# Four-layer scan network on one core: even slots' side work moved ahead of the third exponentials, step sizes made half a block sooner, first and last image's border work put beside the scans

## The chip, the core and the metric

The kernel runs on one core of a Trainium2 chip. A core has five engines that run their own instruction streams in order: TensorE (PE in the profile; its weight loads are PEld), VectorE (DVE), ScalarE (ACT), GpSimd (POOL), and SyncE (SP), which here issues all DMA transfers. Engines wait for each other through semaphores. An instruction that waits holds up everything behind it on its own engine. The metric is the device time of one execution in microseconds (us); lower is better.

## What is computed

Eight images of 48x48 positions and 96 channels pass through four residual layers, each applied to a group-normalized input:

```
x = x + L0(gn(x))   # two-dimensional selective scan, four directions ("ss2d")
x = x + L1(gn(x))   # spectral upsampling, MLP, downsampling
x = x + L2(gn(x))   # selective scans along every row and column ("lines")
x = x + L3(gn(x))   # two-dimensional selective scan again
```

A two-dimensional layer does, per image:

```
xc, z = split(x @ in_proj.T);  xc = silu(depthwise_conv3x3(xc) + conv_b)   # 192 channels
for each of 4 directions k (row-wise, column-wise, and both reversed):
    dts, B, C = split(x_proj[k] @ xs)                  # 6 + 16 + 16 rows
    delta = softplus(dt_proj[k] @ dts + dt_bias[k])
    h = h * exp(delta * A) + (delta * u) * B;  y = sum_n h * C    # 16 states per channel
y = layernorm(sum of the four directions + u * D) * silu(z);  out = y @ out_proj.T
```

The line layer has a four-tap convolution along the line, its own gate and projection per direction, and starts its state at zero on every line.

## The kernel before

**Stages.** `ss2d("l0")`, `spectral`, `lines` and `ss2d("l3")` follow one another. Both kinds of scan layer call the same `scans` (L166).

**Blocks, turns, slots.** Work is a list of blocks (L175): for each image (`job`), for each direction `k`, five pieces of the image, `BLKS`: four of 10 lines (480 columns) and one of 8 (384). A reversed direction takes them from last to first. In the two-dimensional layers directions 0 and 2 run along rows, 1 and 3 along columns; 2 and 3 are reversed. A block has 4 turns (q = 0 to 3), a turn two slots, an even one (2q) and an odd one (2q+1); so a block has `NG` = 8 slots and an image 160. A turn scans 6 units of 128 partitions (channel and state packed), in three scan instructions of two units each.

**A turn, engine by engine** (the loop at L348). ScalarE makes the decays `exp(delta*A)` for two units at a time (`make_da`, L255) into one of two PSUM buffers; a buffer comes free when the scan before last has read it. VectorE runs the three scans (L263) and the products `du*B` (`make_dbu`, L235) for later slots, reading B from one PSUM buffer that ScalarE fills (`copy_b`, L216). GpSimd takes a part of those products (L235), saves the carries between blocks (`keep`, L270) and multiplies the states by C (`make_hc`, L276). TensorE sums over states (`reduce`, L296 and L298); the first reduce of a half-block opens its PSUM group with an `opening` matmul (L292) that reads the running sum of directions, `ysum`. ScalarE copies the finished half back (`done`, L634).

**Side work.** `aside(at)` (L333) is called once in each slot. It issues the next block's loads (`load_bc` in slots 2, 3, 6, 7; `load_dd` in 4, 5), takes one step of the generator `side`, and runs the steps planned for this slot (`run`). In the odd slot it stands after the third scan. In the even slot it stands after the third `make_da`, after `copy_b` and after VectorE's product.

**Planned steps.** `plan(b, at)` (L306) enters the steps that `stage1(b)` returns under their slot numbers. For the two-dimensional layers (L619) these are: the projection to B, C and dts (s0, s1), the store of B and C to DRAM (s3), the two step-size matmuls and bias copies (s4, `biased`), Softplus (s6), `du` on GpSimd for two halves (L422), and two stores of step sizes and du to DRAM (`store_dd`, L410), from where `load_dd` (L192) broadcasts them over partitions. A block is planned two blocks ahead; s0 falls into slot 0, Softplus into slot 6, du into slots 7 and 0, the stores into 1 and 2. The tiles `dds` and `bcl` have one buffer each. Before the loop, 16 slots' worth of planned steps for two blocks run on their own.

**The generator `side` of `ss2d`** (L554): it loads the next image (L468), does `post` of the image before (L496: mean and variance over channels, then Sqrt and reciprocal of all variances, then scaling, gate, output projection and store, block by block), then `front` of the next image (group norm) and, from slot 80 on, `conv` (L470: nine taps on TensorE, one tap group a slot, and two Silu on ScalarE in every eighth slot, 7). For the first image `front` and the whole `conv` run ahead of the scans, and for the last image the whole `post` runs after them.

**The line layer's planned steps** (L774): convolution matmuls in slots 3 and 4, Silu in 6 (L729), step-size matmuls in 7, Softplus in 0 (L757), gate matmuls and du in 1, gate Silu in 2 (L771). So its ScalarE functions other than Exp all fall into even slots. Different functions need different tables, and a load of a table is an instruction of its own in the profile.

Of the kernel before, what the change touches and what calls it, by code (L numbers as in the profile page):

```python
# [16 lines left out]
L = H * W  # L17
# [58 lines left out]
def vss_stack_kernel(ctx: ExitStack, tc: tile.TileContext, i: dict, out: bass.AP):  # L76
# [86 lines left out]
        yield  # L163


    def scans(dirs, restart, a, pools, ps, stage1, opening, done, side, tail):  # L166

# [3 lines left out]


        blocks = [Block(job, k, blk, n == 0, n == len(BLKS) - 1, dirs[k][1])  # L175
                  for job in range(nb) for k in range(NK)
                  for n, blk in enumerate(range(len(BLKS))[::-1 if dirs[k][1] else 1])]
        for b in blocks:
            b.columns(restart)
# [168 lines left out]
        for t, (b, q) in enumerate(turns):  # L348
            at, nblk = 2 * t, t // (NG // 2)
            if q == 0:  # L350
                if nblk + 2 < len(blocks):
                    plan(blocks[nblk + 2], at)
                if b.k == 0 and b.first:
                    beside = side(b.job)
            scan(t, 0)
            if t > 0:
                keep(t - 1, 1)
                make_hc(t - 1, 1)
            make_dbu(at + 2, nc.vector)
# [19 lines left out]
            if q == NG // 2 - 1 and b.k == NK - 1 and b.last:  # L379
                for _ in beside:  # L380
                    while tail:
                        tail.pop(0)()
# [47 lines left out]
    def ss2d(l, xin, xout, b0=0):  # L430
# [36 lines left out]
        def load_x(b):  # L467
            nc.sync.dma_start(xpad[:C, 1:1 + H, 1:1 + W], seq(xin[b], False))  # L468

        def conv(b):  # L470
            us[b] = big.tile([DH, 2, L], F32, tag="big", name="u")
            zs[b] = zdr.tile([DH, 2, L], F32, tag="z", name="zd")
            for r0, nr in BLKS:
                n = nr * SEG
                for half in range(2):
                    pu = side_psum()
# [16 lines left out]
                    yield  # L493
                    nc.sync.dma_start(zs[b][:, half, s], z[:, :n])

        def post(b):  # L496
            y = yss[b]
            var = small.tile([CH, L // CH], F32, tag="var", name="var")
            for r0, nr in BLKS:
# [12 lines left out]
                pv = side_psum()  # L512
                for c in range(n // CH):
                    for half in range(2):
                        nc.tensor.matmul(pv[:CH, c:c + 1], lhsT=sq[:, half, c * CH:(c + 1) * CH], rhs=ones,  # L515
                                         start=(half == 0), stop=(half == 1))
                yield
                nc.vector.tensor_copy(var[:, r0 * W // CH:(r0 * W + n) // CH], pv[:CH, :n // CH])  # L518
                yield
            nc.scalar.activation(var, var, AF.Sqrt, bias=eps5[:CH])  # L520
            yield
            nc.vector.reciprocal(var, var)  # L522
            yield
            for r0, nr in BLKS:
# [124 lines left out]
    def lines(xin, xout):  # L649
# [169 lines left out]
        load_x(0)  # L819
        for _ in front(0):  # L820
            pass
        scans(dirs, True, a, pools, ps, stage1, opening, done, side, tail)
        stack.close()


# [286 lines left out]
```

## Time and profile before

| | us |
|---|---|
| median of 3 runs (lowest to highest) | 19550.73 (19544.21 to 19555.11) |
| the profiled execution, its own time | 19542.61 |
| its span, first to last instruction | 19540.6 |
| first scan of the first layer starts | 148.68 |
| first layer's scans, first to last | 148.7 to 5902.6 |
| last layer's scans, first to last | 13675.7 to 19432.6 |
| last scan to the end | 108.0 |

The mean granted TensorE clock was 0.744 of full speed. The page gives busy time by engine, costliest groups of instructions and who released them. A group's line reads: line of the kernel, engine, operation, output and inputs, shape, count, then busy time, mean duration in ns, then the idle time of the engine just before these instructions and the releasers that ended most of it. A timeline row reads: start, duration, engine, line, operation, tiles, count, and in brackets the idle time before it with its releaser. Idle time of an engine that is not the bottleneck costs nothing. The costliest ScalarE groups beside those shown in the prediction:

```profile
L255 ACT ACTIVATE ps_da<-dd,w_l_a 128x481 f32<-128x481 f32 (+3 forms) x11520 | 7414.7, 648 | 2729.7 <-DVE dbu L263 2523.7
L216 ACT COPY ps_b<-bc 128x480 f32<-128x480 f32 (+1 forms) x3360 | 1798.4, 535 | 300.7 <-DVE dbu L235 271.3
L255 ACT ACT_TABLE_LOAD x970 | 1244.5, 1283 | 17.1
```

### The profile page before, as it was taken

How to read it: one execution, taken by the hardware profiler on the slowest of the kernel's cores; microseconds unless marked ns; L12 is line 12 of the kernel's file. 1: busy time of each engine (PE TensorE's matmuls, PEld its weight loads, DVE VectorE, ACT ScalarE, POOL GpSimd, SP SyncE). 2: the span in 40 equal slices, each digit the busy share in tenths (PEclk: the TensorE clock that was granted, in tenths of full speed). 3: DMA queues.
4: the chain of work that ended last, by engine and by line, in shares of the span. 5: the costliest groups of instructions: out<-in, count | busy, mean ns of one | idle time of the engine just before them, and what ended most of it. 6: DMA issues, size and time to landing. Idle time of an engine off the chain costs nothing. (4 is left out here: it accounts for less than half of the span.)

```text
span 19540.6 us, 172984 instructions
## 1 busy us (share of the span) xinstructions
PE 15237.1 (78%) x53500; PEld 4370.8 (22%) x53500; DVE 16831.8 (86%) x11281; ACT 14144.5 (72%) x22222; POOL 16028.7 (82%) x9825
## 2 busy tenths in 40 slices
PE   6777777777767887888888988887677777777776
PEld 1211211211214552222222222222121121121121
DVE  6999999999992228999999999996999999999997
ACT  5877777877772227788788777885778778778775
POOL 6999999999991007888888888886999999999997
PEclk6777776776767777888878888887677677667765
DMA  3444444444443324434434444443444444444443
GB/s 130 160 162 158 162 160 163 158 163 158 156 170 48 50 45 145 145 141 150 150 139 147 147 146 145 144 149 112 158 163 160 159 164 157 160 162 161 156 165 123
DMA packets 768486, 2829.44 MB, mean 145 GB/s; under 512 B 235724, under 2 KB 298668, under 8 KB 640926
## 3 DMA queue, kind: packets, MB, share of 16 engines
q1 hardware_dynamic: 767558, 2818.38, 43.1%
q8 instruction: 422, 6.91, 0.1%
q14 instruction: 506, 4.15, 0.1%
HBM read 2371.42 MB, written 446.69 MB: 144 GB/s over the span
## 5 line engine op out<-in xcount | busy, mean ns | idle before, releaser
L263 DVE TENSOR_TENSOR_SCAN dbu<-ps_da,dbu 128x962 f32<-128x962 f32 (+3 forms) x5760 | 11858.2, 2071 | 897.9 <-ACT ps_da L255 895.7
L276 POOL TENSOR_TENSOR dbu<-dbu,bc 128x1440 f32<-128x1440 f32 (+1 forms) x3840 | 11439.8, 2985 | 1040.6 <-DVE dbu L263 814.0
L255 ACT ACTIVATE ps_da<-dd,w_l_a 128x481 f32<-128x481 f32 (+3 forms) x11520 | 7414.7, 648 | 2729.7 <-DVE dbu L263 2523.7
L296 PE MATMUL ps_y<-dbu,w_red 128*32 128x480 f32 (+1 forms) x23040 | 4983.6, 752 | 3051.0 <-POOL dbu L276 3047.3
L298 PE MATMUL ps_y<-dbu,w_red 128*32 128x480 f32 (+1 forms) x7680 | 4942.9, 752 | 0.0
L235 DVE TENSOR_TENSOR dbu<-dd,ps_b 128x1440 f32<-128x1440 f32 (+5 forms) x3840 | 4645.3, 1210 | 320.1 <-ACT ps_b L216 275.7
L235 POOL TENSOR_TENSOR dbu<-dd,bc 128x480 f32<-128x480 f32 (+3 forms) x1920 | 3026.2, 1576 | 61.9 <-DMA bc<-bcd 36.6
L296 PEld LDWEIGHTS ps_y<-dbu,w_red 128*32 128x32 f32 x23040 | 742.7, 125 | 7009.7 <-POOL dbu L276 5283.6
L216 ACT COPY ps_b<-bc 128x480 f32<-128x480 f32 (+1 forms) x3360 | 1798.4, 535 | 300.7 <-DVE dbu L235 271.3
L722 PE MATMUL ps_s<-xpad,w_l_cw 128*128 128x480 f32 (+1 forms) x2560 | 1747.2, 834 | 2.3 <-ACT xpad L124 1.6
L481 PE MATMUL ps_side<-xpad,w_l_cw 128*128 128x480 f32 (+1 forms) x2880 | 1617.4, 690 | 4.6 <-ACT xpad L124 4.5
L255 ACT ACT_TABLE_LOAD x970 | 1244.5, 1283 | 17.1
L113 POOL MEMSET w_l_cw<- 128x1760 f32 (+1 forms) x3 | 5.8, 1942 | 1326.7 <-DVE x L932 1321.3
L422 POOL TENSOR_TENSOR dds<-dds,u 96x480 f32<-96x480 f32 (+1 forms) x640 | 793.6, 1240 | 259.9 <-ACT dds L611 259.9
L593 PE MATMUL ps_s<-u,w_l_xp 96*38 96x480 f32 (+1 forms) x1280 | 957.2, 888 | 4.1 <-ACT dds L587 3.0
L583 PE MATMUL ps_s<-bcl,dtw 6*96 6x480 f32 (+1 forms) x1280 | 878.4, 775 | 86.3 <-ACT dds L587 82.2
L270 POOL COPY carry<-dbu 128x3 f32<-128x3 f32 x2048 | 386.4, 189 | 582.6 <-DVE dbu L263 570.2
L292 PE MATMUL ps_y<-ysum,w_ident 96*96 96x480 f32 (+1 forms) x960 | 740.7, 861 | 113.7 <-ACT ysum L634 112.8
L481 PEld LDWEIGHTS ps_side<-xpad,w_l_cw 128*128 128x128 f32 x2880 | 571.0, 222 | 1115.0 <-issue 916.4
L722 PEld LDWEIGHTS ps_s<-xpad,w_l_cw 128*128 128x128 f32 x2560 | 525.8, 210 | 1087.1 <-issue 938.1
L298 PEld LDWEIGHTS ps_y<-dbu,w_red 128*32 128x32 f32 x7680 | 683.1, 125 | 0.0
L763 PE MATMUL ps_s<-xpad,w_l_inz 96*96 96x480 f32 (+1 forms) x640 | 505.7, 924 | 86.9 <-ACT dds L757 69.2
(146 smaller groups left out, 12586.2 us busy)
## 6 DMA issues: line engine op xcount, KB each, us to landing
dd<-dd SPq DMA_DIRECT2D x512, 1443.0 KB
bc<-bcd SPq DMA_DIRECT2D x1536, 480.0 KB
dd<-dd SPq DMA_DIRECT2D x256, 1440.0 KB
dd<-dds SPq DMA_DIRECT2D x512, 360.8 KB
dd<-dd SPq DMA_DIRECT2D x128, 1155.0 KB
bc<-bcd SPq DMA_DIRECT2D x384, 384.0 KB
dd<-dds SPq DMA_DIRECT2D x256, 360.0 KB
dd<-dd SPq DMA_DIRECT2D x64, 1152.0 KB
```

Source lines behind the costliest of these rows:

```text
L216: nc.scalar.copy(bps[t][:, :b.n], bcs[t][:, 0, :b.n])
L235: engine.tensor_mul(o, du, by.unsqueeze(1).to_broadcast([P, hi - lo, b.n]))
L255: nc.scalar.activation(da[:, at:at + b.m], b.got[half][:, u % 3, 0, :], AF.Exp, scale=a[:, b.k, ci:ci + 1])
L263: nc.vector.tensor_tensor_scan(db, da, db, 0.0, ALU.mult, ALU.add)
L276: nc.gpsimd.tensor_mul(h, h, bcs.pop(2 * t + sub)[:, 1, :n].unsqueeze(1).to_broadcast([P, 3, n]))
L296: nc.tensor.matmul(y[32 * g:32 * g + 32, :n], lhsT=wc["red"][:, :32], rhs=hc[:, g, b.at], start=False, stop=(slot == 3))
L298: nc.tensor.matmul(y[DH:, :n], lhsT=wc["red"][:, 32:], rhs=hc[:, 2, b.at], start=(slot == 0), stop=(slot == 3))
L422: nc.gpsimd.tensor_mul(rows(du, n), rows(dt, n), u)
L481: nc.tensor.matmul(pu[:, :n], lhsT=flat[:, at:at + P], rhs=xpad[:, r0 + dy:r0 + dy + nr, dx:dx + W], start=(tap == 0), stop=(tap == 8))
L583: nc.tensor.matmul(got["p"][:DH, :n], lhsT=dtw[2 * NS:, b.k, half, :], rhs=b.bcl[2 * NS:, :n], start=True, stop=True)
L593: nc.tensor.matmul(got["p"][:NBC, :n], lhsT=w[f"{l}_xp"][:, b.k, half, :], rhs=u[:, half], start=(half == 0), stop=(half == 1))
L722: nc.tensor.matmul(got["u", half][:, :n], lhsT=flat[:, at:at + P], rhs=shifted(off), start=(tap == 0), stop=(tap == 3))
```

## The change

Five edits. In `scans`: (a) the order of directions becomes an argument; the two-dimensional layers use 0, 1, 3, 2, the line layer the old one. (b) Blocks are planned three ahead, with base slot `at + NG`, and three blocks' planned steps run before the loop instead of two. (c) In the even slot, `reduce` and `aside` move ahead of `copy_b`, the third `make_da` and VectorE's product. In `ss2d`: (d) the keys of `stage1` go down by four, so that each step falls four slots (half a block) earlier relative to its block's scans: s0 in slot 4, Softplus in slot 2, du in 3 and 4, stores in 5 and 6. In the line layer keys and base cancel, and steps keep their slots. (e) `conv` and `post` take a list of blocks. The first image's last convolution block goes into `side`, two steps a slot; the last image's `post` goes into `side` block by block for four of the five blocks, two steps a slot, each once its rows are complete, and only one block is left after the scans. Each such `post` has a Sqrt and a reciprocal of its own.

```diff
         blocks = [Block(job, k, blk, n == 0, n == len(BLKS) - 1, dirs[k][1])
-                  for job in range(nb) for k in range(NK)
+                  for job in range(nb) for k in order
...
-        for n, b in enumerate(blocks[:2]):
+        for n, b in enumerate(blocks[:3]):
             plan(b, NG * (n - 2))
-        for t in range(-2 * NG, 0):
+        for t in range(-3 * NG, 0):
             run(t)
...
             if q == 0:
-                if nblk + 2 < len(blocks):
-                    plan(blocks[nblk + 2], at)
-                if b.k == 0 and b.first:
+                if nblk + 3 < len(blocks):
+                    plan(blocks[nblk + 3], at + NG)
+                if b.k == order[0] and b.first:
                     beside = side(b.job)
...
             scan(t, 1)
-            make_da(t, 2)
-            copy_b(at + 3)
-            make_dbu(at + 3, nc.vector)
             if t > 0:
                 reduce(t - 1, 1)
             aside(at)
+            copy_b(at + 3)
+            make_da(t, 2)
+            make_dbu(at + 3, nc.vector)
             bring(t + 1)
...
         def side(job):
             used = 0
             more = job + 1 < nb
+            if job == 0:
+                for n, _ in enumerate(conv(0, BLKS[4:])):
+                    if n % 2:
+                        used += 1
+                        yield
             if more:
                 load_x(job + 1)
...
-                yield from conv(job + 1)
+                yield from conv(job + 1, BLKS)
+            else:
+
+                for n, blk in enumerate(BLKS[:0:-1]):
+                    while used < (NK * len(BLKS) - len(BLKS) + n + 1) * NG + 2:
+                        used += 1
+                        yield
+                    for m, _ in enumerate(post(job, [blk])):
+                        if m % 2:
+                            used += 1
+                            yield
...
-            return {0: s0, 1: s1, 3: s3, 4: s4, 5: lambda: biased(1), 6: s6, 7: du(0), 8: du(1),
-                    NG + 1: store(0), NG + 2: store(1)}
+            return {-4: s0, -3: s1, -1: s3, 0: s4, 1: lambda: biased(1), 2: s6, 3: du(0), 4: du(1),
+                    5: store(0), 6: store(1)}
...
-        for _ in conv(0):
+        for _ in conv(0, BLKS[:4]):
             pass
-        scans(dirs, False, a, pools, ps, stage1, opening, done, side, [])
-        for _ in post(nb - 1):
+        scans(dirs, (0, 1, 3, 2), False, a, pools, ps, stage1, opening, done, side, [])
+        for _ in post(nb - 1, BLKS[:1]):
             pass
```

More of the change, by code (lines that the diff above doesn't have):

```diff
@@ L163, in norm_scale, with scans @@
         yield
-    def scans(dirs, restart, a, pools, ps, stage1, opening, done, side, tail):
+    def scans(dirs, order, restart, a, pools, ps, stage1, opening, done, side, tail):
         blocks = [Block(job, k, blk, n == 0, n == len(BLKS) - 1, dirs[k][1])
-                  for job in range(nb) for k in range(NK)
+                  for job in range(nb) for k in order
                   for n, blk in enumerate(range(len(BLKS))[::-1 if dirs[k][1] else 1])]
@@ L378, in scans @@
             aside(at + 1)
-            if q == NG // 2 - 1 and b.k == NK - 1 and b.last:
+            if q == NG // 2 - 1 and b.k == order[-1] and b.last:
                 for _ in beside:
@@ L468, in load_x, with conv @@
             nc.sync.dma_start(xpad[:C, 1:1 + H, 1:1 + W], seq(xin[b], False))
[L470 to L473, printed above, removed]
+        def conv(b, blks):
+            if blks[0] == BLKS[0]:
+                us[b] = big.tile([DH, 2, L], F32, tag="big", name="u")
+                zs[b] = zdr.tile([DH, 2, L], F32, tag="z", name="zd")
+            for r0, nr in blks:
                 n = nr * SEG
@@ L494, in conv, with post @@
                     nc.sync.dma_start(zs[b][:, half, s], z[:, :n])
-        def post(b):
+        def post(b, blks=BLKS):
             y = yss[b]
             var = small.tile([CH, L // CH], F32, tag="var", name="var")
-            for r0, nr in BLKS:
+            v0, v1 = min(r0 for r0, nr in blks) * W // CH, max(r0 + nr for r0, nr in blks) * W // CH
+            for r0, nr in blks:
                 n = nr * SEG
@@ L519, in post @@
                 yield
-            nc.scalar.activation(var, var, AF.Sqrt, bias=eps5[:CH])
+            nc.scalar.activation(var[:, v0:v1], var[:, v0:v1], AF.Sqrt, bias=eps5[:CH])
             yield
-            nc.vector.reciprocal(var, var)
+            nc.vector.reciprocal(var[:, v0:v1], var[:, v0:v1])
             yield
-            for r0, nr in BLKS:
+            for r0, nr in blks:
                 n = nr * SEG
@@ L821, in lines @@
             pass
-        scans(dirs, True, a, pools, ps, stage1, opening, done, side, tail)
+        scans(dirs, range(NK), True, a, pools, ps, stage1, opening, done, side, tail)
         stack.close()
```

## The prediction

> **What bounds the kernel now.** I read the page first (busy shares, costliest groups), then VectorE's waits in the first scan stage, then timelines of single blocks, then both ends of a stage.
>
> ```profile
> PE 15237.1 (78%) x53500; PEld 4370.8 (22%) x53500; DVE 16831.8 (86%) x11281; ACT 14144.5 (72%) x22222; POOL 16028.7 (82%) x9825
> L263 DVE TENSOR_TENSOR_SCAN dbu<-ps_da,dbu 128x962 f32<-128x962 f32 (+3 forms) x5760 | 11858.2, 2071 | 897.9 <-ACT ps_da L255 895.7
> L276 POOL TENSOR_TENSOR dbu<-dbu,bc 128x1440 f32<-128x1440 f32 (+1 forms) x3840 | 11439.8, 2985 | 1040.6 <-DVE dbu L263 814.0
> ```
>
> VectorE (DVE) and GpSimd (POOL) carry the scan stages. What VectorE loses there is one wait, the scan for its exponentials (third number after the bar). The starts of every twelfth scan in the timeline give block times: in both two-dimensional stages a 480-column block takes 34.5 to 34.8 us without a convolution beside it (last image, second half), and 36.7 with one. VectorE's own work is 34.2 (turns of 8.3 and 8.8 us where no wait is shown); GpSimd's is 34.8 (timeline from 5633 us, where it is never idle: eight products at a pitch of 3.28 with their carry copy, four B products 6.3, two du 2.25). So GpSimd is the floor, 0.6 above VectorE, and a convolution block wastes 1.9. Here is one, on ScalarE (ACT) and VectorE:
>
> ```profile
> 2007.94 0.56 ACT L216 COPY ps_b<-bc 128x480 f32<-128x480 f32 x1 [0.18 <-DVE dbu L235]
> 2008.52 1.28 ACT L611 ACT_TABLE_LOAD   x1
> 2009.82 1.00 ACT L611 ACTIVATE dds<-dds 96x960 f32<-96x960 f32 x1
> 2010.93 1.28 ACT L255 ACT_TABLE_LOAD   x1
> 2012.22 1.36 ACT L255 ACTIVATE ps_da<-dd,w_l_a 128x481 f32<-128x481 f32 x2
> 2014.08 1.28 ACT L490 ACT_TABLE_LOAD   x1
> 2016.51 1.28 ACT L255 ACT_TABLE_LOAD   x1
> ```
> ```profile
> 2013.62 2.16 DVE L263 TENSOR_TENSOR_SCAN dbu<-ps_da,dbu 128x962 f32<-128x962 f32 x1 [0.53 <-ACT ps_da L255]
> 2019.20 2.16 DVE L263 TENSOR_TENSOR_SCAN dbu<-ps_da,dbu 128x962 f32<-128x962 f32 x1 [1.88 <-ACT ps_da L255]
> ```
>
> Softplus (slot 6) and the convolution's Silu (slot 7) follow each other, each with two table loads: the scans wait 0.53 and 1.88 us. In the line stage the waits are for Silu, Softplus, Silu in slots 6, 0 and 2, and TensorE (PE) is late:
>
> ```profile
> 9606.81 7.75 PE L722 MATMUL ps_s<-xpad,w_l_cw 128*128 128x480 f32 x8
> 9614.60 0.66 ACT L729 ACTIVATE ub<-ps_s,w_l_cb 96x480 f32<-96x480 f32 x1 [0.26 <-PE ps_s L722]
> ```
>
> The convolution of this column block ended 6.5 us after its turn's first scan (9608.08), and ScalarE, which came 5.6 us after it, still waited. At the ends of a stage nothing is hidden:
>
> ```profile
> 127.32 5.44 SPq L192 DMA_DIRECT2D dd<-dd  x2
> 132.30 0.66 ACT L587 ACTIVATE dds<-ps_s,w_l_dtb 96x480 f32<-96x480 f32 x1 [14.08 <-DMA dd<-dds]
> ```
> ```profile
> 19446.82 0.16 DVE L518 COPY var<-ps_side 96x5 f32<-96x5 f32 x1 [4.10 <-PE ps_side L515]
> 19483.02 0.16 DVE L518 COPY var<-ps_side 96x4 f32<-96x4 f32 x1 [3.75 <-PE ps_side L515]
> 19493.17 0.65 DVE L550 TENSOR_TENSOR xi<-xi,ps_side 96x480 f32<-96x480 f32 x1 [5.91 <-PE ps_side L547]
> ```
>
> **What the Trainium skill says.** "ScalarE: Activation LUTs", What ACT_TABLE_LOAD costs: a change of table set is 1283 ns plus a drain of 1380. The trace has the 1283 (1.28 above), not the drain: loads start 0.02 us after the copy before. "SBUF — State Buffer", SBUF: two separate sides: a VectorE instruction with two SBUF inputs and a GpSimd instruction exclude each other for their whole length. The trace agrees: L149, a 96x1 subtraction, takes 0.15 us with GpSimd idle and 2616 ns on average beside the scans. The pieces of post read one operand from PSUM, so I charge no lock. "DMA: Bandwidth & Descriptors", the SWDGE anatomy: most of a transfer's fixed 2 us is the write's receipt. Here the store of the step sizes costs block 1 a wait of 14.08 us, far more, and that number is used.
>
> **1. Softplus moved from slot 6 to 2 (plan a block earlier, keys four lower).** Convolution blocks: with no Softplus before it, the slot-7 chain starts when the second scan of turn 3 ends: from the start of the exponentials (2012.22) to the end of the next ones (2019.16) it is 6.95 us; the second scan of the next turn is naturally 6.6 after that start. Left: 0.4 instead of 0.53+1.88. In exchange Softplus now heads the even slot of turn 1: ScalarE ends the turn's second exponentials about 1.6 us (row blocks) to 2.0 (columns, whose ysum copy takes 0.97, not 0.55) after the first scan's start, as in turn 3 today (5624.42 against 5622.78); then load 1.29, Softplus 1.0, the B copy 0.5, load 1.29, exponentials 1.36: 5.45. The third scan is due at 6.72. Stall 0.3 to 0.7, in convolution blocks some 0.9 since ScalarE is still catching up. I add 0.2 for GpSimd's burst of du in turn 2, which holds TensorE's reduce and so the bcl copy. So 34.2+0.4+0.9+0.2 = 35.7: 1.0 saved per 480 block; the 384 block, 32.9 now, to 27.8 of VectorE's work and the same two stalls before shorter scans, 1.2 and 1.6, 30.6: 2.3; the first block of the next image 1.0. Eight, one and one: 11.3 per image, 7 images, 2 stages: **-158**. Bounds: 0 (stall only moved) to 21 per image (GpSimd's floor). The moved steps' stores come along: bcd in slot 7, dd in slots 5 and 6, now on SP behind that slot's load_bc or load_dd, seven slots ahead of their own reload instead of three; no wait for dd is shown in this stage, so nothing is gained, and SP has no work that waits on them for long: 0. Other blocks: 0.53 becomes 0.3 to 0.8; about 160 of them at +0.1: **+16** (-30 to +60).
>
> **2. Even slot's side work first, in the line stage.** SP and GpSimd keep their order here; ScalarE and VectorE change. Odd slots hold only the bcl copy, so the chain starts 0.9 us after the first scan in turns 3 and 1, 1.65 in turn 0. Plus load 1.29, two functions 1.25, B copy (not before 3.65), load, exponentials: ready at 6.85, 6.8 and, in turn 0, 7.25, against 6.72, 6.72 and 6.2 (its VectorE product is 0.63, not 1.13). Stalls 0.15+0.1+1.05 = 1.3 a block, against 1.83 of first-scan waits now (1.07+0.71+0.05 by turn, from VectorE's idle before each scan); the add's wait for project shrinks little. Row blocks gain about 0.6: 80 of them, -50. In column blocks the Silu must wait for the convolution, 4.0 to 6.5 us after the first scan, and behind Silu stand the B copy and the third exponentials: the stall is that lateness minus 2.9. TensorE then waits back (bcl copy 0.7 later, gated later than its opening), up to 1.5 a block; with the faster matmuls of other blocks I take 0.9: 80 times, +70. Together **+20** (-50 to +150).
>
> **3. Last image's post beside scans.** Today the first loop of post runs from 19446.8 to 19483.0 after its first block, and the second from 19493.8 (first add) to 19540.6. With one block left: 19446.98, then load and Sqrt 1.6 (partly under the matmuls), reciprocal, and the 10 us from reciprocal to add: end near 19460 with its store. 80 per stage: **-160**. The four blocks move to the last four scan blocks, two steps a slot, so producer and consumer meet in one slot. VectorE: 1.15+0.16+0.27+1.4+0.65 = 3.6; stalls: 0.6 (mean matmul behind the reduce), 3 (Sqrt waits for the variance copy after the second scan, then B copy, load, exponentials follow), 1 (add behind GpSimd's product and two matmuls). 8.2 by 4 by 2: **+66** (30 to 110). GpSimd hides its 2.2 each: no du is left there.
>
> **4. First image.** One convolution block less ahead: 13.5 us (two halves of 6.7). But three blocks are planned before the loop, and load_dd of block 0 now stands on SP's queue behind block 1's stores, whose du waits for the 14.08 us above. Shifted by 13.5, those du end at 125.6 where the loads are issued at 127.3 now. First scan about 1 us earlier: **-2** in all. Without that queue it would be -25. Beside: two Silu groups in slots 3 and 7, 2.5 us; then the load of image 1 is released only after slot 7 and bn_stats stands in VectorE's order: the load takes 10 us (7.3 to 17.2), cover about 4: 6. **+18**.
>
> **5. Order 0, 1, 3, 2.** Same sizes and counts; each opening is still a turn behind its last copy: 0. It is what allows part 3.
>
> Sum: -158+16+20-160+66-2+18 = **-200** on the span of 19540.6; the median stands 10 above it: 19350.
>
> **Rivals.** *GpSimd's floor is reached* (0.22): the stalls of part 1 disappear in slack. Per image 8 x 1.9+3.4+2.5 = 21.1, x14 = -295; lines -50; other blocks 0; with borders -78: -423, 19125. For it: job 7's blocks run at 34.8 with Softplus present; against: ScalarE is in order and full in turns 0 and 1. *Slower* (0.16): ScalarE enters turn 1's even slot late. The ysum copy and the second biased of slot 1 wait for TensorE, in order behind GpSimd's product; "ACT bcl L598 <- PE ps_s L593" is 457.9 us over 219 times, 2.1 each, and today such a wait stands before slack. Now each microsecond of it delays B copy, product and third scan of 320 Softplus blocks: +320. It decides from 0.6 us; at 1.5 it is +480: 19830. Against: 1.64 measured in turn 3 holds the same two operations. *No change* (0.06): lines +150 and Softplus +60 eat the gain.
>
> **How the numbers follow.** Forecast 0.56, floor 0.22, slower 0.16, no change 0.06. 0.2% (39 us) is what a measurement of this kernel tells from no change. Forecast and floor are faster: 0.78; same 0.06; slower 0.16. The range 19110 to 19540 reaches to the floor and to just under the time before, leaving the slower case out; the forecast's own is 19230 to 19480.
>
> **What would show it.** Convolution blocks at 35.7 (34.8: floor; 36.7: stall moved); VectorE's wait for L255 mainly before third scans; "ACT ub <- PE" grown from 34.6 us (within 8162 to 12750) to hundreds; last scan to end 28 us instead of 108; first scan still near 148; last image's final four blocks near 43. Wrong if line blocks pass 40 or third scans wait over 1.5 us in every block.

## The result, and the profile after

The change makes the kernel slower: 19815.37 us (median of 4 runs, 19802.64 to 19840.51) against 19552.92 (19544.21 to 19568.71) on the same chip, ratio 1.0135 with a 95% interval of 1.0117 to 1.0152. Forecast was 19350. The profiled execution has a span of 19800.9 against 19540.6 before, at a granted clock of 0.752 against 0.744, so a lower clock is not the cause.

First where the 260 us of span are. From the starts and ends of the scans in the timeline, in us:

| part of the span | before | after | difference |
|---|---|---|---|
| start to first scan, first layer | 148.7 | 155.5 | +7 |
| scans of the first layer | 5754.0 | 5872.3 | +118 |
| last scan to first scan of the line stage | 1495.0 | 1438.8 | -56 |
| scans of the line stage | 6120.9 | 6271.7 | +151 |
| to first scan of the last layer | 157.2 | 165.3 | +8 |
| scans of the last layer | 5757.0 | 5866.3 | +109 |
| last scan to the end | 108.0 | 30.9 | -77 |

So the borders gave what they were to give, and all three scan stages lost. Groups of the page after, in the order of the page (L605 is `biased`, L587 before; the other lines have their old numbers):

```profile
L263 DVE TENSOR_TENSOR_SCAN dbu<-ps_da,dbu 128x962 f32<-128x962 f32 (+3 forms) x5760 | 11811.7, 2068 | 942.2 <-ACT ps_da L255 914.9
L276 POOL TENSOR_TENSOR dbu<-dbu,bc 128x1440 f32<-128x1440 f32 (+1 forms) x3840 | 11441.9, 2983 | 1138.2 <-DVE dbu L263 946.7
...
L235 DVE TENSOR_TENSOR dbu<-dd,ps_b 128x1440 f32<-128x1440 f32 (+5 forms) x3840 | 4649.5, 1211 | 670.9 <-ACT ps_b L216 645.3
...
L235 POOL TENSOR_TENSOR dbu<-dd,bc 128x480 f32<-128x480 f32 (+3 forms) x1920 | 3022.6, 1574 | 612.9 <-DMA bc<-bcd 537.2
...
L605 ACT ACTIVATE dds<-ps_s,w_l_dtb 96x480 f32<-96x480 f32 (+1 forms) x640 | 406.8, 636 | 636.7 <-DMA dd<-dds 504.4
```

Two of these groups before the change:

```profile
L235 DVE TENSOR_TENSOR dbu<-dd,ps_b 128x1440 f32<-128x1440 f32 (+5 forms) x3840 | 4645.3, 1210 | 320.1 <-ACT ps_b L216 275.7
L235 POOL TENSOR_TENSOR dbu<-dd,bc 128x480 f32<-128x480 f32 (+3 forms) x1920 | 3026.2, 1576 | 61.9 <-DMA bc<-bcd 36.6
```

Busy times and mean durations are nearly those of before; what changed is the third part of the lines, the idle time. The scans wait for exponentials about as much as before (898 us then). But three waits have grown: VectorE's products wait for the B copy (671 against 320), GpSimd's products wait for a transfer, the load of B and C (613 against 62), and the bias copies wait for another, the store of the step sizes (637 against 79). The forecast charged nothing for either transfer.

SyncE's issues around the start of a block in the last image, first before (a block starts at 5597.40 and the next at 5632.18), then after (5676.06); start, duration, queue, line, operation, tiles:

```profile
5597.35 0.74 SPq L410 DMA_DIRECT2D dd<-dds  x1
5598.14 0.53 SPq L204 DMA_DIRECT2D bc<-bcd  x1
5603.09 0.71 SPq L410 DMA_DIRECT2D dd<-dds  x1
5603.84 0.57 SPq L204 DMA_DIRECT2D bc<-bcd  x1
5605.54 0.31 SPq L601 DMA_DIRECT2D bcd<-bcl  x1
5607.66 6.67 SPq L192 DMA_DIRECT2D dd<-dd  x2
5623.68 3.81 SPq L204 DMA_DIRECT2D bc<-bcd  x2
```
```profile
5670.51 0.54 SPq L204 DMA_DIRECT2D bc<-bcd  x1
5671.10 0.72 SPq L410 DMA_DIRECT2D dd<-dds  x1
5673.22 0.53 SPq L204 DMA_DIRECT2D bc<-bcd  x1
5673.84 1.84 SPq L619 DMA_DIRECT2D bcd<-bcl  x1
5677.08 3.21 SPq L204 DMA_DIRECT2D bc<-bcd  x2
```

Each block loads B and C in four pieces. Before, pieces three and four (5623.68, x2) were issued with nothing between them, eight and five us ahead of the block that uses them. After, the store of the second half of the step sizes (L410) stands between them. What the fourth piece meets in the new block, ScalarE, GpSimd and VectorE in order of time:

```profile
5681.32 0.66 ACT L605 ACTIVATE dds<-ps_s,w_l_dtb 96x480 f32<-96x480 f32 x1 [3.77 <-DMA dd<-dds]
5682.41 0.56 ACT L216 COPY ps_b<-bc 128x480 f32<-128x480 f32 x1 [0.44 <-DMA bc<-bcd]
5682.47 2.04 POOL L235 TENSOR_TENSOR dbu<-dd,bc 128x960 f32<-128x960 f32 x1 [2.71 <-DMA bc<-bcd]
...
5683.01 0.66 DVE L235 TENSOR_TENSOR dbu<-dd,ps_b 128x480 f32<-128x480 f32 x1 [1.19 <-ACT ps_b L216]
...
5684.37 4.21 DVE L263 TENSOR_TENSOR_SCAN dbu<-ps_da,dbu 128x962 f32<-128x962 f32 x2 [0.71 <-ACT ps_da L255]
```

The store issued at 5671.10 landed at about 5681.3, 10.2 us later, and the load issued 2.1 us behind it landed at about 5682.4, 9.2 us after its own issue. Two engines waited for it, ScalarE with its B copy and GpSimd, and behind the B copy product and scan came late.

The trace also has each DMA packet and each increment of a transfer's semaphore, and they show how the load came to be so late. The core has 16 DMA engines and a load's semaphore is incremented 16 times; I take each increment for one engine's share, and the packets below agree. Thirteen increments of this load came at 5676.38 to 5676.83, 3.2 to 3.6 us after its issue; the last three at 5680.85, 5680.87 and 5682.33. The store in front of it is not spread like that: its 96 packets of 3848 bytes run in three rows side by side, from 5674.06 to 5680.84, and its last three increments came at 5679.72, 5679.73 and 5681.16. Of the load's 128 packets of 3840 bytes, 104 (thirteen sixteenths) start by 5676.4; the other 24 start when the store's rows are through, two rows near 5679.4, the third at 5680.85. The packet records don't name the engine; that these are the same three is read from these times. So the load waits for three sixteenths of its data, which stand in line behind the store's packets on three engines. The Trainium skill states ("DMA: Bandwidth & Descriptors", Queues, rings and completion order) that a semaphore increment lands only after every earlier write of the same DMA engine. The trace agrees: the load's three late increments come 1.1 to 1.2 us behind the store's three. But the increments are not all that is late; the packets themselves are.

That a store takes ten microseconds could be seen before: the `load_dd` at 5607.66 needed the store issued at 5597.35, 10.3 us earlier. The same lateness was there too: before the change the first and second pieces were issued right behind a store (5598.14 and 5603.84 above), and in a window of the first layer (900 to 5250 us) their last increment came 10.6 and 11.6 us after the issue (medians). But they were issued 33 and 29 us ahead of their block; the fourth piece of the changed kernel has 4.1.

In the line stage the blocks that carry a column block's convolution went from 38.5 to 40.2 us (means over the middle six images); the others stayed at 38.2 to 38.3. A turn 3 there, TensorE, ScalarE, VectorE:

```profile
8587.54 7.75 PE L740 MATMUL ps_s<-xpad,w_l_cw 128*128 128x480 f32 x8
...
8595.33 0.66 ACT L747 ACTIVATE ub<-ps_s,w_l_cb 96x480 f32<-96x480 f32 x1 [4.62 <-PE ps_s L740]
8595.88 0.56 ACT L216 COPY ps_b<-bc 128x480 f32<-128x480 f32 x1
...
8596.47 1.15 DVE L235 TENSOR_TENSOR dbu<-dd,ps_b 128x960 f32<-128x960 f32 x1 [2.47 <-ACT ps_b L216]
...
8599.21 4.20 DVE L263 TENSOR_TENSOR_SCAN dbu<-ps_da,dbu 128x960 f32<-128x960 f32 x2 [1.59 <-ACT ps_da L255]
```

The convolution is still running when ScalarE comes for the second half of its Silu: 4.62 us of waiting. In the new order the B copy, VectorE's odd product (2.47 late) and the third scan (1.59 late) stand behind that wait; before, they stood ahead of it.

At the end of the program, VectorE after its last scans (the post of the one block that is left):

```profile
19780.82 1.15 DVE L510 TENSOR_TENSOR ysum<-ysum,ps_side 96x960 f32<-96x960 f32 x1 [7.06 <-PE ps_side L507]
...
19786.17 0.16 DVE L521 COPY var<-ps_side 96x5 f32<-96x5 f32 x1 [4.19 <-PE ps_side L518]
...
19788.95 1.33 DVE L541 SCALAR_TENSOR_TENSOR ysum<-ysum,w_l_nw,ps_side 96x480 f32<-96x480 f32 x2 [2.07 <-PE ps_side L537]
```

One pass of the two loops instead of five: 30.9 us from the last scan to the end, where it was 108.

### The profile page after: what moved, and what is told of

It is laid out like the page before. It is cut to its first block, busy times and chain, and to the rows that moved or that the text cites. A ratio compares the mean times of both kernels' runs of the same rounds, so it can differ in the third digit from the quotient of the medians.

```text
span 19800.9 us, 175329 instructions
## 1 busy us (share of the span) xinstructions
PE 15289.3 (77%) x53500; PEld 4367.6 (22%) x53500; DVE 16888.3 (85%) x11289; ACT 14104.0 (71%) x22254; POOL 16016.8 (81%) x9825
## 4 chain that ended last, share of the span: by engine, by line
POOL 30%; DVE 20%; PE 16%; ACT 12%; DMA 11%; issue 10%; SPq 0%; POOLq 0%; DVEq 0%; ACTq 0%
POOL dbu L276 21%; DVE dbu L263 13%; DMA bc<-bcd 9%; DVE dbu L235 5%; POOL dbu L235 4%; ACT ps_da L255 4%; POOL dds L422 3%; PE ps_s L740 3%; ACT L255 2%; PE ps_y L296 2%; PE ps_h L970 2%; PE ps_y L983 1%; ACT ps_b L216 1%; PE ps_s L812 1%; PE ps_side L482 1%
## 5 line engine op out<-in xcount | busy, mean ns | idle before, releaser
L296 PE MATMUL ps_y<-dbu,w_red 128*32 128x480 f32 (+1 forms) x23040 | 5075.4, 765 | 2756.6 <-POOL dbu L276 2753.4
L298 PE MATMUL ps_y<-dbu,w_red 128*32 128x480 f32 (+1 forms) x7680 | 5034.6, 765 | 0.0
L601 PE MATMUL ps_s<-bcl,dtw 6*96 6x480 f32 (+1 forms) x1280 | 906.3, 798 | 451.0 <-ACT z L493 349.1
L605 ACT ACTIVATE dds<-ps_s,w_l_dtb 96x480 f32<-96x480 f32 (+1 forms) x640 | 406.8, 636 | 636.7 <-DMA dd<-dds 504.4
L768 PE MATMUL ps_s<-bcl,dtw 6*96 6x480 f32 (+1 forms) x640 | 449.6, 843 | 407.6 <-ACT bcl L762 407.6
```

What stands on the lines that cost most here:

```text
L296: nc.tensor.matmul(y[32 * g:32 * g + 32, :n], lhsT=wc["red"][:, :32], rhs=hc[:, g, b.at], start=False, stop=(slot == 3))
L298: nc.tensor.matmul(y[DH:, :n], lhsT=wc["red"][:, 32:], rhs=hc[:, 2, b.at], start=(slot == 0), stop=(slot == 3))
L601: nc.tensor.matmul(got["p"][:DH, :n], lhsT=dtw[2 * NS:, b.k, half, :], rhs=b.bcl[2 * NS:, :n], start=True, stop=True)
```

## The experiments

Two theories at first. *Queue theory*: the sooner step sizes changed what stands ahead of the B and C loads, by the stores on SyncE's queue and by GpSimd's earlier `du`, which stand ahead of the products that free the B/C buffers; the line stage loses separately, by the new even slot. *Even-slot theory*: side work ahead of the third exponentials costs in all stages, and the transfers are late only as a consequence. A third theory, the forecast's own rival for "slower", is that ScalarE comes late in turn 1 because its copies wait for TensorE.

### The three parts, each alone on the kernel before

`sooner_only` has (b) and (d) of the change, `even_only` (c), `borders_only` (a) and (e) (with blocks still planned three ahead, but the keys on their old slots).

```diff
# sooner_only: keys and plan as in the change, even slot and borders as before
+            return {-4: s0, -3: s1, -1: s3, 0: s4, 1: lambda: biased(1), 2: s6, 3: du(0), 4: du(1),
+                    5: store(0), 6: store(1)}
# even_only
-            make_da(t, 2)
-            copy_b(at + 3)
-            make_dbu(at + 3, nc.vector)
             if t > 0:
                 reduce(t - 1, 1)
             aside(at)
+            copy_b(at + 3)
+            make_da(t, 2)
+            make_dbu(at + 3, nc.vector)
# borders_only, against the changed kernel: these two undone
```

> The kernel before with only the step sizes made half a block sooner (plan a block earlier, keys four lower); even slots, order of the directions and borders as before. Queue theory (the moved du and stores make GpSimd's releases of the B/C buffers later and put the stores behind SP's loads): slower by 80 to 250 us, all of it in the two two-dimensional stages (each scan stage +40 to +125), with GpSimd waiting for bc loads about 1.5 us a block and ScalarE for the store of dds; the line stage unchanged within 15 us. Even-slot theory (only the place of the side work ahead of the third exponentials costs): no slower than before, -100 to 0 us.

> The kernel before with only the even slot's side work ahead of the B copy, the third exponentials and the odd product. Queue theory: the line stage as in the changed kernel, +130 to +170 us; the two-dimensional stages within 60 us of before in sum: ratio 1.004 to 1.012. Even-slot theory: the two-dimensional stages lose here what they lose in the changed kernel, +200 us, beside the lines' +150: ratio 1.016 or more.

> The changed kernel with the old keys of the step sizes and the old even slot: the order 0, 1, 3, 2 and the border work of first and last image beside scans remain. Both theories: between -110 and +10 us, likeliest -50: the ends of the two stages lose 130 to 160, four blocks with a piece of post each cost 6 to 10 us a block twice, the first image's blocks 10 to 20 twice.

| | median | ratio [95%] | scans of first layer | line scans | last layer | ends |
|---|---|---|---|---|---|---|
| sooner | 19660.62 | 1.0056 [1.0041, 1.0071] | +39 | -10 | +43 | first scans 21 and 23 later |
| even slot | 19744.58 | 1.0096 [1.0081, 1.0111] | +14 | +171 | +11 | +5 in all |
| borders | 19472.91 | 0.9957 [0.9943, 0.9972] | +52 | -7 | +48 | first scans 14 and 13 sooner, line stage 62 sooner, end 77 sooner |

The columns are differences of the profiled executions to before. The spans add up: +121, +201 and -72 make +250, and the changed kernel has +260. With the step sizes in their old place the even-slot theory is out for the two-dimensional stages (+25 together), and it is right for the lines. The sooner step sizes lose by themselves, with the old even slot, and show the same wait: "POOL dbu <- DMA bc<-bcd" is 564 us on its page. ScalarE's wait for the store, expected as well, is not among its waits in the window; it waits for the load there (154.9 us).

### What makes the B and C loads late

First the store's own wait. In `dds_once` the step sizes' tile is taken once for the stage; then the first bias copy waits for the store of its own half only.

```diff
+        dds = pools["dds"].tile([DH, 2, 2 * WMAX], F32, tag="dds", name="dds")
...
-                b.dds = pools["dds"].tile([DH, 2, 2 * WMAX], F32, tag="dds", name="dds")
+                b.dds = dds
```

> The changed kernel with the step sizes' tile kept for the whole stage instead of taken anew for each block, so that the first biased copy waits for the store of half 0 alone, and the second (a slot later) for that of half 1. Queue theory: the wait of the first biased copy for a store (505 us by the page) falls below 100, and the time falls by 60 to 200 us against the changed kernel (ratio to before 1.003 to 1.010); GpSimd's wait for bc stays. Rival (ScalarE is late in turn 1 because its copies wait for TensorE): no change, ratio 1.011 to 1.015.

19826.84 us, ratio 1.0138 [1.0121, 1.0155]: nothing came back, and the queue theory as stated missed. ScalarE's waits in a window of the first layer (900 to 5250 us), changed kernel first, then this one; line waited for, us in total, times, longest:

```profile
ACT dds L605 <- DMA dd<-dds: 168.8, 85, 4.8
...
ACT ps_b L216 <- DMA bc<-bcd: 69.7, 93, 4.6
```
```profile
ACT ps_b L216 <- DMA bc<-bcd: 254.4, 96, 5.5
```

The wait for the store is gone, and the B copy behind it now stands the same time for its load. The store had only covered a load that was just as late. The runs that follow act on that load.

```diff
# bc8: 8 buffers in the two-dimensional stages; sq takes zin's buffer and xi has one, for room
-        free = {n: 0 for n in range(NBUF)}
+        free = {n: 0 for n in range(NBUF if restart else 8)}
# bc8_dds: bc8 and dds_once together
# loads_last: in aside, the block of load_bc and load_dd moved behind next(beside) and run(at)
# best1: bc8_dds with the old even slot in all stages
# borders_bc8: borders_only with the 8 buffers
```

> The changed kernel with 8 instead of 6 B/C buffers in the two-dimensional stages (room from two tiles of post that share one buffer, and one xi buffer instead of two). Queue theory: GpSimd's wait for bc (537 us by the changed kernel's page) falls below 120; the first biased copy's wait for the store of dds (505 us) stays and is now the last one, so only part comes back: 20 to 150 us less than the changed kernel, ratio to before 1.005 to 1.012. Rival (the B/C loads are late because SP holds them behind the stores, not for want of a free buffer): GpSimd's wait stays over 300 us, ratio 1.012 to 1.015.

> 8 B/C buffers and the step sizes' tile kept for the whole stage, both on the changed kernel. Queue theory: both DMA waits are gone, the blocks with a convolution of the two-dimensional stages fall from 36.7 to 35.5 to 36.3 us, and each of these stages is 60 to 200 us shorter than in the changed kernel: ratio to before 0.996 to 1.007. Rival (ScalarE in turn 1's even slot is what is late, whatever the DMAs do): blocks stay at 36.5 or more, ratio 1.010 to 1.015.

> The changed kernel with a slot's loads issued after its steps on SP's queue, so that the stores of the step sizes and of B and C stand ahead of the next block's loads. Queue theory (buffer late because of GpSimd's moved products): the store lands earlier, the first biased copy's wait for it falls below 150 us, but the B/C loads are released no earlier and GpSimd's wait for them stays over 300 us; the time moves by less than 60 us. Rival (order on SP): GpSimd's wait falls below 150, and 80 to 250 us come back.

> The changed kernel with the old even slot in all stages, 8 B/C buffers and the kept tile of step sizes: borders and sooner step sizes without their DMA waits. Queue theory: lines as before (6115 us of scans), the two-dimensional scan stages 5700 to 5800 us against 5805 with the borders alone: ratio 0.988 to 0.996. If the sooner Softplus gains nothing even without the DMA waits: 0.9955 to 0.998.

> Borders alone, with 8 B/C buffers in the two-dimensional stages and neither the sooner step sizes nor the new even slot. If the buffers only pay for the lateness that the sooner step sizes bring: as the borders alone, ratio 0.994 to 0.998. If the buffers themselves were what shortened the stages: 0.987 to 0.992, as with the sooner step sizes.

| | median | ratio [95%] | two-dimensional scan stages |
|---|---|---|---|
| 8 buffers | 19611.08 | 1.0038 [1.0023, 1.0053] | 5777, 5763 |
| 8 buffers, kept tile | 19606.08 | 1.0034 [1.0021, 1.0047] | 5785, 5780 |
| loads last | 20541.0 | 1.0512 [1.0496, 1.0528] | 6224, 6227 |
| 8 buffers, kept tile, old even slot | 19324.7 | 0.989 [0.9874, 0.9907] | 5728, 5726 |
| borders, 8 buffers | 19463.19 | 0.9955 [0.994, 0.997] | 5806, 5807 |

GpSimd's wait for the loads in the window, changed kernel first, then `bc8`:

```profile
POOL dbu L235 <- DMA bc<-bcd: 188.0, 89, 5.3
```
```profile
POOL dbu L235 <- DMA bc<-bcd: 44.9, 24, 4.8
```

With eight buffers it falls from 188 to 45 us, and 200 us come back, slightly more than the 20 to 150 expected. The tile of step sizes is worth nothing here either. The buffers alone, without the sooner step sizes, are worth nothing (`borders_bc8` equals `borders_only`), so they only repair what the sooner step sizes break. The old even slot is then worth 280 us; by the spans 191 of it lie in the line scans and 57 and 54 in the two-dimensional scans. So there the new even slot does cost something, but mostly together with the sooner step sizes, which put Softplus into turn 1's even slot.

`loads_last` missed both expectations by far. SyncE works in order: with the steps ahead, it stands at a store that has no data yet while the loads behind it already have their buffers. Its waits for Softplus, and ScalarE's for loads, in the window:

```profile
SPq L410 <- ACT dds L629: 826.4, 94, 11.2
```
```profile
ACT ps_b L216 <- DMA bc<-bcd: 534.3, 102, 12.8
```

Pieces three and four also stand behind a store again: their last increments come 10.2 and 8.3 us after the issue (medians).

Eight buffers let the fourth load be issued 9.8 us ahead of its block (median) instead of 4.1, so they can't tell a late release from a store in front. `store_late` can: `dds_once` with one key changed, so that the store is issued behind the fourth load; the release stays.

```diff
-                    5: store(0), 6: store(1)}
+                    5: store(0), 7: store(1)}
```

> The version with the kept tile of step sizes, with the store of half 1 a slot later, so that on SP's queue it stands behind the fourth B/C load of the next block and not between the third and the fourth. The buffers are released as before. If the store's transfer ahead of that load makes it late: GpSimd's wait for bc falls from 191 us (window 900 to 5250) below 80, the time falls 80 to 200 us, ratio 1.003 to 1.010. If the late release of the buffer alone does: the wait stays over 140 us, ratio 1.011 to 1.016 or more, since the second biased copy now waits longer for its store.

19600.23 us, ratio 1.0026 [1.0015, 1.0037]; slightly more came back than the 80 to 200 us expected. SyncE's issues around piece four (a block starts at 5614.89), now a load pair and then the store:

```profile
5608.79 3.79 SPq L204 DMA_DIRECT2D bc<-bcd  x2
5612.63 0.72 SPq L410 DMA_DIRECT2D dd<-dds  x1
```

GpSimd's longest waits in the window, `dds_once` first, then `store_late`:

```profile
POOL dbu L235 <- DMA bc<-bcd: 190.7, 87, 4.4
POOL carry L270 <- DVE dbu L263: 97.3, 124, 1.9
```
```profile
POOL carry L270 <- DVE dbu L263: 210.6, 237, 3.3
POOL dbu L276 <- DVE dbu L263: 58.2, 59, 2.1
```

The load wait is gone from the window (71.4 us are left on the page, 550.5 in `dds_once`), though the load is issued no more than 0.4 us sooner. GpSimd again waits for scans, as before the change. The semaphore records of the fourth load, medians over the window, in us:

| | issued ahead of its block | 13th increment after the issue | 16th and last |
|---|---|---|---|
| before | 5.7 | 3.3 | 3.6 |
| changed kernel | 4.1 | 3.7 | 9.2 |
| `dds_once` | 3.9 | 3.5 | 9.3 |
| `bc8` | 9.8 | 3.7 | 10.7 |
| `store_late` | 4.3 | 3.6 | 3.8 |

In the changed kernel the 14th increment comes over 1.5 us behind the 13th in 154 and 156 of 159 blocks of the two stages; before, and in `store_late`, in none. Eight buffers leave the load as late and only issue it sooner. So it is the order of a store and a load on one queue, and not the release of a buffer, that cost 227 us (19826.84 less 19600.23). By the spans, all of it lies in the two-dimensional scans: 106 and 121 us.

### The line stage

In `even_conv` the two convolution halves of the line stage go a slot ahead, so that TensorE has finished when Silu comes. In `even_not3` the new even slot is used in turns 0 to 2 of the line stage only.

```diff
# even_conv: even_only and
-            return {3: conv(0), 4: conv(1), 6: s2s3, 7: s5, 8: s6, 9: s7, 10: s8, 11: lambda: store_dd(b, 1)}
+            return {2: conv(0), 3: conv(1), 6: s2s3, 7: s5, 8: s6, 9: s7, 10: s8, 11: lambda: store_dd(b, 1)}
# even_not3: before, and the moved calls stand behind aside(at) where
+            sooner = restart and q < NG // 2 - 1
```

> The kernel before with the new even slot, and in the line stage the two halves of the convolution a slot earlier (slots 2 and 3 instead of 3 and 4). Theory: in column blocks ScalarE's Silu heads the even slot of turn 3 and waits for the convolution, so its wait for TensorE (183 us in the window from 8200 to 12500 us with the new even slot) falls below 80, column blocks fall from 40.6 to 38.5 to 39.5, and the line scans from 6292 to between 6130 and 6230: ratio 1.001 to 1.007. Rival (the chain behind any Silu is too long, wherever the convolution stands): ratio 1.008 or more.

> The kernel before with the new even slot in turns 0 to 2 of the line stage alone; turn 3 and the two-dimensional stages as before. Theory: the column blocks' stalls of turn 3 (3.2 us a block) go, the old wait before the first scan of turn 0 (0.75 in row blocks, 1.4 in column blocks) comes back, and turn 0 keeps its 1.3 before the third scan: line scans 6160 to 6230, ratio 1.002 to 1.006. Rival (turn 0 is the loss): lines still over 6260, ratio 1.007 or more.

`even_conv`: 20189.45 us, 1.0327 [1.0309, 1.0344]; a miss in time. `even_not3`: 19649.89 us, 1.0049 [1.0034, 1.0064], line scans 6206.8, as expected. VectorE's idle time before its instructions, us per block, worked out from the timelines of the middle six images ("column" blocks carry a column block's convolution):

| | row: 1st scan | row: turn 0, 3rd | row: turns 1 and 3, 3rd | row: add | column: 1st scan | column: turn 0, 3rd | column: turn 3, product and 3rd | column: add |
|---|---|---|---|---|---|---|---|---|
| before | 1.39 | 0 | 0 | 0.68 | 2.29 | 0 | 0 | 0.77 |
| even_only | 0 | 1.43 | 0.62 | 0.22 | 0 | 1.25 | 3.22 | 0.37 |
| even_conv | 0 | 1.36 | 0.64 | 2.08 | 0 | 1.52 | 0.34 | 5.87 |
| even_not3 | 0.76 | 2.03 | 0.31 | 0 | 1.01 | 1.87 | 0 | 0 |

The mechanism holds for turn 3: with the convolution a slot ahead turn 3's stall in column blocks falls from 3.22 to 0.34. But the convolution now stands ahead of `project` on TensorE, and VectorE's add waits for that. Its waits for it in a window of the line stage (8200 to 12500 us), `even_only` first, then `even_conv`:

```profile
DVE x L802 <- PE ps_s L794: 24.8, 33, 1.0
```
```profile
DVE x L802 <- PE ps_s L794: 343.5, 73, 7.0
```

Leaving turn 3 alone brings back half the loss; the rest is turn 0, where Softplus stands ahead of the third scan whatever the block.

### A version that beats both

`best3` is `best1` with the loads of block 0 issued ahead of block 1's stores in the part before the loop. `best4` is that with 6 buffers, as in the kernel before, and the late store; `best5` has both the late store and 8 buffers.

```diff
         for t in range(-3 * NG, 0):
+            if t == -3:
+                for half in range(2):
+                    load_dd(blocks[0], half)
+                for n in range(4):
+                    load_bc(n)
             run(t)
-        for half in range(2):
-            load_dd(blocks[0], half)
-        for t in range(4):
-            load_bc(t)
```

> The version with old even slot, 8 B/C buffers and kept tile of step sizes, and the loads of the first block issued ahead of the second block's stores. Expected: the first scan of a two-dimensional stage 15 to 25 us earlier each, 30 to 50 us in all, ratio 0.9855 to 0.989.

> Borders, sooner step sizes and early loads of the first block, old even slot, with 6 B/C buffers and the store of half 1 behind the fourth B/C load. If the place of that store is the whole of what the 8 buffers repaired: as with the 8 buffers, ratio 0.9855 to 0.9895. If the later release of the buffers costs as well: 0.990 to 0.995.

> The same with 8 B/C buffers beside the later store. If the place of the store is the whole: within 0.15% of the version with 6 buffers. If the release costs as well: 0.3% or more below it.

`best3`: 19294.58 us, 0.9871 [0.9857, 0.9886]; the first scans come 17 and 18 us sooner than in `best1`. `best4`: 19263.08 us, 0.9857 [0.984, 0.9873]. `best5`: 19260.1 us, 0.9853 [0.9839, 0.9868]: with the store in its place the number of buffers makes no difference, so the release has no part in it that can be measured. `best4` is 290 us faster than before, needs no memory that the kernel before did not use, and keeps of the change the borders and the sooner step sizes, not the new even slot.

## Why the prediction was wrong

**Part 1, the step that failed.** The forecast said that the stores come along, "now on SP behind that slot's load_bc or load_dd", that "no wait for dd is shown in this stage, so nothing is gained, and SP has no work that waits on them for long: 0". It asked who waits for SyncE, and not who waits for the transfers that SyncE issues behind the stores. The term was -142 for both stages (-158 and +16); the part alone cost +82 in the scans and +44 ahead of them, and in the changed kernel the scans are 66 and 61 us above `borders_only`. `store_late` shows the missing term, 227 us. It was also not true that no wait for a store was shown. VectorE had none in this stage and ScalarE one of 0.6 us, but SyncE's own waits before the change, in the window, have this:

```profile
SPq L192 <- DMA dd<-dds: 751.1, 202, 7.5
```

Each load of step sizes stood until a store had landed, ten microseconds after its issue. Those waits were harmless in their place. The forecast knew a figure of 14.08 us for such a store from the start of a stage and used it only there.

With the store in its place, the rest of part 1 holds with the old even slot: from `borders_only` to `best4` the scan stages fall by 104 and 99 us, more than the 71 each that were forecast, and the last convolution blocks of an image take 35.0 to 35.8 us, where 35.7 was forecast and 36.7 is the time before. With the new even slot (`store_late`), which is what the forecast was made for, they fall by 34 and 42 only, 66 us short. Its mechanism is there: in the eight 480-column convolution blocks of an image VectorE idles 0.38 us before the second scan of turn 0 (0.4 forecast) and 0.90 before the third scan of turn 1 (0.9 forecast), where it was 0.83 before the first scan and 1.86 before the second in turn 0. These blocks take 35.9 us. Most of what is missing is the 384-column block among them, forecast at 30.6 us: it takes 33.6, more than the 32.9 before, which makes some 40 us over 7 images in 2 stages.

**Part 2, mis-sized.** Forecast +20 for the line stage (row blocks -50, column blocks +70); measured +151 in the changed kernel and +171 alone. Row blocks: the forecast had stalls of 1.3 us a block against 1.83, which is the mean over row blocks (1.39) and column blocks (2.29); they are 2.05 (1.43 in turn 0, 0.62 in the two others) against 1.39, and the savings on the add's wait (0.46) and on a wait for the load of step sizes (0.21) just balance that: 0 instead of -50. The largest piece, turn 0, was forecast at 1.05. Column blocks: the forecast charged turn 3's lateness once, with 0.9 us a block over the row blocks. It falls twice, on the odd product (1.77) and then on the third scan behind it (1.45), since the B copy and the exponentials both stand behind Silu. Their blocks lose 2.1 us, 80 times: +168.

**Part 3, close.** Forecast -160 at the two ends and +66 beside the scans. Measured alone: -77 at the end, -62 ahead of the line stage, and the last image's job +37 and +35; -67 in sum against -94. The last four blocks took 45.6, 46.0, 43.0 and 40.0, near 43 as said. No run separates the order of the directions (part 5, forecast 0) from this.

**Part 4, right in its mechanism.** The forecast said that block 0's loads stand behind block 1's stores, and that it would be -25 without that queue. First scans came 7 and 8 us later where -2 was forecast, and early loads give 17 and 18 us. Beside the scans, the first image's job costs 6 and 7 us alone, forecast 9 each.

**The rivals.** The rival on the slower side put 19830, near the measured time, but its mechanism is not what cost that: it had the second bias copy and the ysum copy wait for TensorE. In the window "ACT dds <- PE ps_s" is 28.7 us for 119 blocks, and the bcl copy's wait for TensorE fell from 176.9 to 115.9. With the store moved (`store_late`) the first of these waits is 80.5 us, so a part of the mechanism is there once the transfers are in time. The total is near 19830 by accident; the loss lies in transfers and in the line stage. GpSimd's floor was not reached; GpSimd waited for transfers. Of the signs named in advance, three were right (waits before third scans, "ACT ub <- PE" at 173.9 instead of 34.6, the end at 30.9). The first scan, said to stay near 148, came at 155.5. Convolution blocks at 36 to 37 us gave the sign for "stall moved", and of the two signs of being wrong one came, line blocks over 40 (40.2, those with a column block's convolution).

## What to carry to other kernels

When a step is moved, list its transfers and look at each neighbour in the issuing queue: a load issued behind a store can be as late as the store, even if nothing it reads depends on it, because it has landed only when its last share has. So stores go behind the loads that are needed first, and slack decides: the same lateness cost nothing 30 us ahead of a block and 227 us in total 4 us ahead of it. Read the issuing queue's own waits too; those of the compute engines showed next to nothing of this before the change. When a wait goes away and the time stays, look at the next instruction of the same engine: here a second transfer was just as late, and only the run that moved one store told a late buffer from a store in front. Side work may go ahead of a time-critical chain only if its own inputs are early and the chain has room for it: Silu ahead of the third exponentials carried TensorE's lateness to VectorE twice, and Softplus in turn 0 cost 1.4 us a row block.

## What the runs showed of the hardware that was not expected

A store of 361 KB to DRAM took 10.2 to 10.3 us from its issue until a wait for it ended, and a load of 480 KB issued 2.1 us behind it ended 9.2 us after its own issue, because the store ran on three of the 16 DMA engines and three sixteenths of the load stood behind it there; the other thirteen had landed 3.6 us after the issue. Most of the store's ten microseconds are therefore no fixed cost of a transfer: its 96 packets alone run for 6.8 us on three engines. With the store behind the load the last share lands after 3.8 us (median), the others after 3.6. Why the store runs on three engines no run shows; its access pattern in `store_dd` (L410) has three groups outermost (`g=3`), and a store of another shape was not tried.

Putting the loads of a slot behind its steps on SyncE, with the same transfers in all, took 3.7% more than the changed kernel (20541.0 against 19815.37 us). An order of the even slot that changed no amount of work made the line scans 2.8% longer (171 of 6121 us).
